# A four-layer graph network on one core: a first stage with a hand-written order, R held as two reduced-precision rows, both attention scores from one product

## The chip, the cores and the metric

The kernel runs on one core of one Trainium2 chip. The time is the device time of one execution in microseconds; of several runs the median is given. Every trace is that of one further, profiled execution, whose own time stands beside its span.

## What is computed

A stack of four layers over a graph of N = 3327 nodes with 512 features. The adjacency matrix is an N x N array of integers with about half a per cent of ones. Layers 0, 2 and 3 are graph attention with 8 heads of 64 features, layer 1 is a SAGE layer (mean of the neighbours); each is applied to relu(layernorm(x)) and added to x. Cut to what matters, a layer of attention is:

```python
h   = maximum(layernorm(x), 0)
Wh  = (h @ W).reshape(n, H, F)
f1  = einsum('nhf,hf->nh', Wh, a1)          # score of the destination
f2  = einsum('nhf,hf->nh', Wh, a2)          # score of the source
e   = leaky_relu(f1[:, None, :] + f2[None, :, :], 0.2)
e   = where(adj[:, :, None] > 0, e, -9e15)
out = einsum('ijh,jhf->ihf', softmax(e, axis=1), Wh)
x   = x + elu(out)                          # layer 0: batch norm and relu instead
```

and layer 1 is

```python
agg = mask @ h / maximum(deg, 1)
x   = x + relu(concat([h @ W_self + b_self, agg @ W_nb + b_nb]) @ W_comb + b_comb)
```

## The kernel before

Nodes are padded to 3328 and taken in 26 blocks of 128 rows; the destinations are taken in 52 groups of 64 (GB). Since few edges exist, each group has a list of source nodes, the union of the neighbours of its 64 nodes, and only those rows are gathered.

**A weight without the leaky relu.** Since exp(leaky_relu(f1 + f2)) is the larger of exp(f1 + f2) and exp(0.2 (f1 + f2)), a weight of the softmax is, up to a factor that the softmax removes, the larger of R(destination) = exp(0.8 f1 + a constant) and a value of the source, times exp(f2). exp(f2) is multiplied into the features beforehand. So a table row of a source (v_row, written to `table`) holds, for each head, exp(f2) x Wh, exp(f2) itself, and the value that is compared; `r_dram` holds R.

**The first stage** (0 to about 355 us) is the function `lists`, which also runs the projection of layer 0 (`Projection.block`, `Norms.block`) and the products of the weights with the attention vectors (`Products.layer`, L477 and L478). For each of the 26 blocks of rows of the adjacency matrix, DVE compares the integers with zero and counts them (L878, adj_b), PE packs them into words (26 small products, L882, words_ps), ACT copies the words (L883) and DVE takes two maxima (L885, which groups have which sources). After two of every three blocks one block of the projection follows: its normalisation (L764 to L770 on DVE, L779 on ACT), four transposes (L782, h_ps), relu (L785, hT), two score products (L593, with the destination scores as rows; L595 with the source scores as columns; sd_ps), the product with W (L597, wh_ps), the exponentials (L600, L601, L605), the clamp (L604) and the multiplication of a row (L610). After blocks 5 and 11 come the weight products of layers 2 and 3. Then the marks are transposed (L906 and L909, cnt), a scan (L912) and 11 steps, one for each bit (L918 to L921), turn them into lists of sources, each step followed by one of the remaining blocks of the projection; L926 and L927 end this. The lists go to DRAM and come back in another layout (L940 and L950, half on SP's queue, half on ACT's), and are put into an index array (L960 to L972). The first gather of layer 0 reads `idx` and `table`. What runs when on each engine is set by the scheduler here, which takes the order of the program as a guide.

**Attention** (`attend`, three times) has a fixed order on PE, DVE and ACT. The sources of a group come in units of three chunks of 128. POOL gathers rows for the next unit (L1019); for each group PE spreads R over the partitions (`spread`, L1052, r_bc: a product of a row of 512 with a column of ones), fetched two groups ahead on SP's queue (L1044, r_one); DVE takes the maximum (L1120, mx) and multiplies with the mask (L1127, wgt); PE accumulates the products of weights and rows (L1141, facc; about 110 a group). When a group is complete, `ending` divides and writes it out in steps, one step per unit (`later`), and the same call ticks whatever runs beside.

**Beside** layer 0 run products of weights for the later SAGE layer (fwx_ps, fb_ps) and sums for the batch norm (bmean_ps). Beside SAGE runs the projection of layer 2, beside layer 2's attention that of layer 3: class `Following`. Its `tick` advances the oldest block that is ready by one step, and all early ones (norm). A block has four steps in `rest`: transposes and relu (p_ps L710, hT L713); scores (p_sd, L717 and L719) with the exponentials L722 and L723 and a copy of the destination scores (L725); the clamp (L728) and the product with W (p_wh, L731); the exponential of R, its DMA and the multiplication of the rows (L733 to L739). All its tiles in PSUM share one tag with `pb` buffers, 2 beside SAGE and 1 beside layer 2's attention. What is left at the end of a stage is worked off by `drain`.

Of the kernel before, what the change touches and what calls it, by code (L numbers as in the profile page):

```python
# [24 lines left out]
BF16 = mybir.dt.bfloat16  # L25
I32 = mybir.dt.int32
# [10 lines left out]
P = 128  # L37
H = 8
F = 64
# [414 lines left out]
class Products:  # L454
# [4 lines left out]
    def __init__(self, tc, t, pool, wp, wps):  # L459
        self.nc, self.t, self.wp, self.wps = tc.nc, t, wp, wps  # L460
        self.WA = []
        for l in range(3):
            WA = pool.tile([P, KC, 2 * H], F32, name=f"WA{l}")
            self.WA.append(WA)
        self.ok = pool.tile([1, 1], I32, name="ok")

    def layer(self, l):
# [3 lines left out]
        nc.scalar.dma_start(Wt, t[wn].rearrange("(kc p) o -> p kc o", p=P))  # L471
        for k, an in enumerate((ai, aj)):
            ab = wp.tile([P, D], F32, name="wa_bc", tag="wa_bc", bufs=2)
            nc.scalar.dma_start(ab, t[an].partition_broadcast(P))
            for kc in range(KC):
                pr = wp.tile([P, D], F32, name="wa_pr", tag="wa_pr", bufs=2)
# [5 lines left out]
    def bound(self):  # L482
# [9 lines left out]
        ps = self.wps.tile([P, 3, 2 * H], F32, name="wa_n")  # L492
# [78 lines left out]
class Projection:  # L571
# [4 lines left out]
    last, pb = "wh_ps", 1  # L576

    def __init__(self, tc, cs, N, wl, xin, W, WA, table, r_dram, pool, psum, hb=2):
# [6 lines left out]
        self.norms = Norms(tc, cs, pool, psum, xin, hb)  # L585

    def block(self, c):
        nc, pp, pps, WA, wl = self.tc.nc, self.pool, self.psum, self.WA, self.wl
        hT = self.norms.block(c, self.hs)
        wh = pps.tile([P, D], F32, name="wh_ps", tag="wh_ps", bufs=1)  # L590
        sd = pps.tile([P, BANK], F32, name="sd_ps", tag="sd_ps", bufs=1)
        for kc in range(KC):
            nc.tensor.matmul(sd[:, :H], hT[:, kc, :], WA[wl][:, kc, H:], start=(kc == 0), stop=(kc == KC - 1))  # L593
        for kc in range(KC):
            nc.tensor.matmul(sd[:H, P : 2 * P], WA[wl][:, kc, :H], hT[:, kc, :], start=(kc == 0), stop=(kc == KC - 1))  # L595
        for kc in range(KC):
            nc.tensor.matmul(wh, hT[:, kc, :], self.Wt[:, kc, :], start=(kc == 0), stop=(kc == KC - 1))  # L597
        row = pp.tile([P, ROW], F32, name="v_row", tag="v_row", bufs=3)
        V = row[:, : H * (F + 1)].rearrange("p (h f) -> p h f", f=F + 1)
        nc.scalar.activation(V[:, :, F : F + 1], sd[:, :H].rearrange("p (h o) -> p h o", o=1), AF.Exp)  # L600
        nc.scalar.activation(row[:, H * (F + 1) :], sd[:, :H], AF.Exp, scale=-0.8, bias=self.cs["down"])  # L601

        rr = pp.tile([H, P], F32, name="r_row", tag="r_row", bufs=2)
        nc.vector.tensor_scalar(rr, sd[:H, P : 2 * P], -SMALL, SMALL, ALU.max, ALU.min)  # L604
        nc.scalar.activation(rr, rr, AF.Exp, scale=0.8, bias=self.cs["down"][:H])  # L605
        n = P // GB
        nc.sync.dma_start(
            self.r_dram[c * n : (c + 1) * n, :, :].rearrange("g h i -> h g i"), rr.rearrange("h (g i) -> h g i", i=GB)
        )
        nc.vector.tensor_tensor(  # L610
            V[:, :, 0:F], wh.rearrange("p (h f) -> p h f", f=F), V[:, :, F : F + 1].to_broadcast([P, H, F]), ALU.mult
        )
        nc.sync.dma_start(self.table[c * P : (c + 1) * P, :ROW], row.bitcast(I32))
# [39 lines left out]

class Following:
# [15 lines left out]
    def tick(self):  # L670
        if self.ready and next(self.ready[0], None) is None:
            self.ready.pop(0)
        for g in list(self.early):
            hx = next(g)
            if hx is not None:
                self.early.remove(g)
                self.ready.append(self.rest(*hx))
# [28 lines left out]
    def rest(self, c, hx):  # L706
# [9 lines left out]
        for kc in range(KC):  # L716
            nc.tensor.matmul(sd[:, :H], hT[:, kc, :], WA[wl][:, kc, H:], start=(kc == 0), stop=(kc == KC - 1))  # L717
        for kc in range(KC):
            nc.tensor.matmul(sd[:H, P : 2 * P], WA[wl][:, kc, :H], hT[:, kc, :], start=(kc == 0), stop=(kc == KC - 1))  # L719
        row = pp.tile([P, ROW], F32, name="v_row", tag="v_row", bufs=2)  # L720
        V = row[:, : H * (F + 1)].rearrange("p (h f) -> p h f", f=F + 1)
        nc.scalar.activation(V[:, :, F : F + 1], sd[:, :H].rearrange("p (h o) -> p h o", o=1), AF.Exp)  # L722
        nc.scalar.activation(row[:, H * (F + 1) :], sd[:, :H], AF.Exp, scale=-0.8, bias=self.cs["down"])  # L723
        rr = pp.tile([H, P], F32, name="r_row", tag="r_row", bufs=2)
        nc.scalar.copy(rr, sd[:H, P : 2 * P])  # L725
        yield True

        nc.vector.tensor_scalar(rr, rr, -SMALL, SMALL, ALU.max, ALU.min)  # L728
        wh = self.psum.tile([P, D], F32, name="p_wh", tag="p_ps", bufs=self.pb)
        for kc in range(KC):  # L730
            nc.tensor.matmul(wh, hT[:, kc, :], self.Wt[:, kc, :], start=(kc == 0), stop=(kc == KC - 1))  # L731
        yield True
        nc.scalar.activation(rr, rr, AF.Exp, scale=0.8, bias=self.cs["down"][:H])  # L733
        n = P // GB
        nc.sync.dma_start(
            self.r_dram[c * n : (c + 1) * n, :, :].rearrange("g h i -> h g i"), rr.rearrange("h (g i) -> h g i", i=GB)
        )
        for h in range(H):
            nc.scalar.mul(V[:, h, 0:F], wh[:, h * F : (h + 1) * F], V[:, h, F : F + 1])  # L739
        nc.sync.dma_start(self.table[c * P : (c + 1) * P, :ROW], row.bitcast(I32))  # L740
        yield None


class Norms:


    def __init__(self, tc, cs, pool, psum, xin, hb):
        self.__dict__.update(locals())
        self.NB = xin.shape[0] // P
        self.have = {}  # L750

# [726 lines left out]
```

## Time and profile before

| | us |
|---|---|
| three runs | 3010.09, 2994.06, 2988.13 |
| median | 2994.06 |
| the profiled execution, its own time | 3035.44 |
| its span, first to last instruction | 3033.2 |
| its mean granted TensorE clock | 0.788 |

| stage, from the trace | us |
|---|---|
| adjacency loop: first compare starts, last compare ends | 24.9, 252.3 |
| final shift of the lists ends (L927) | 338.3 |
| first gather of layer 0 | 355.4 |
| layer 0's attention | 355 to 945 |
| batch norm and own part of SAGE | 945 to 1120 |
| SAGE with the projection of layer 2 | 1120 to 1733 |
| layer 2's attention with the projection of layer 3 | 1733 to 2430 (from 2386 the drain) |
| layer 3's attention | 2440 to 3033 |

How to read the lines shown below. PE is TensorE (products), PEld its loading of weights, DVE VectorE, ACT ScalarE, POOL GpSimd, SP SyncE, which issues DMAs. A row of digits divides the span into 40 slices, and each digit is the busy share in tenths; PEclk is the clock that was granted to TensorE, in tenths of the full one. The chain of waits follows back from the last instruction what released each piece; "issue" is time in which an engine waited for nothing that the profile shows. A line of a group reads: line, engine, operation, output<-inputs, shapes, xcount, then busy time in us and the mean of one in ns, then the idle time of the engine before them and what ended it. A line of the waits reads: engine, its line, what it waited for, then us in total, number, longest. A line of the windows reads: window, its length, busy us (and number of instructions) of PE, PEld, DVE, ACT and POOL, then the clock, the DMA engines' share and GB/s.

### The profile page before, as it was taken

How to read it: one execution, taken by the hardware profiler on the slowest of the kernel's cores; microseconds unless marked ns; L12 is line 12 of the kernel's file. 1: busy time of each engine (PE TensorE's matmuls, PEld its weight loads, DVE VectorE, ACT ScalarE, POOL GpSimd, SP SyncE). 2: the span in 40 equal slices, each digit the busy share in tenths (PEclk: the TensorE clock that was granted, in tenths of full speed). 3: DMA queues.
4: the chain of work that ended last, by engine and by line, in shares of the span. 5: the costliest groups of instructions: out<-in, count | busy, mean ns of one | idle time of the engine just before them, and what ended most of it. 6: DMA issues, size and time to landing. Idle time of an engine off the chain costs nothing.

```text
span 3033.2 us, 55483 instructions
## 1 busy us (share of the span) xinstructions
PE 2335.1 (77%) x22046; PEld 1441.9 (48%) x22046; DVE 1797.3 (59%) x2124; ACT 1051.0 (35%) x3857; POOL 1376.2 (45%) x1464
## 2 busy tenths in 40 slices
PE   4767577878787786888988677888889757777775
PEld 2434244555554332333333355555665445656554
DVE  7657577778876910011111277777766367887886
ACT  1223112233334322344444313445666601223333
POOL 1000255556551046666554255555544056565553
PEclk9778788877778898799999767777777766676766
DMA  7563377776662746666655366666655166666664
GB/s 279 186 258 125 133 217 226 235 222 207 201 191 78 248 140 198 195 202 221 202 182 180 114 169 183 186 181 188 185 173 171 56 184 186 188 195 194 200 197 130
DMA packets 186637, 561.52 MB, mean 185 GB/s; under 512 B 35385, under 2 KB 40321, under 8 KB 183044
## 3 DMA queue, kind: packets, MB, share of 16 engines
q0 software_dynamic: 114880, 404.47, 45.4%
q1 hardware_dynamic: 68470, 148.32, 13.8%
q10 hardware_dynamic: 3022, 5.11, 0.5%
q8 instruction: 177, 2.90, 0.4%
q14 instruction: 88, 0.72, 0.1%
HBM read 498.42 MB, written 59.36 MB: 184 GB/s over the span
## 4 chain that ended last, share of the span: by engine, by line
PE 63%; issue 14%; ACT 5%; DVE 2%; another core or an unknown queue 2%; DMA 1%; POOL 1%; SPq 0%; DVEq 0%; ACTq 0%; POOLq 0%
PE facc L1141 29%; PE p_wh L731 7%; PE r_bc L1052 6%; PE sage_acc L1376 5%; PE n_ps L1325 3%; PE p_sd L719 2%; PE p_sd L717 2%; PE s_ps L1300 2%; PE fwx_ps L1218 1%; PE bmean_ps L1228 1%; PE p_ps L710 1%; ACT v_row L739 1%; POOL rows L1019 1%; PE a_ps L1319 1%
## 5 line engine op out<-in xcount | busy, mean ns | idle before, releaser
L1019 POOL DMA_INDIRECT rows<-table,idx x1077 | 1025.4, 952 | 1231.6 <-PE facc L1141 362.4
L1141 PE MATMUL facc<-rows,wgt 128*64 128x65 f32 x17232 | 953.3, 270 | 380.9 <-issue 342.1
L1141 PEld LDWEIGHTS facc<-rows,wgt 128*64 128x64 f32 x17232 | 826.1, 178 | 669.3 <-issue 556.4
L1127 DVE TENSOR_TENSOR wgt<-mx,mask 128x1536 f32<-128x1536 f32 (+1 forms) x405 | 638.3, 1576 | 174.4 <-PE facc L1141 82.4
L1120 DVE TENSOR_TENSOR mx<-r_bc,rows 128x1536 f32<-128x1536 f32 (+1 forms) x405 | 639.5, 1579 | 163.9 <-PE facc L1141 75.9
L1019 POOL DMA_INDIRECT z_rows<-h_dram,idx x359 | 341.2, 950 | 392.0 <-ACT hT L1297 139.2
L1079 ACT ACTIVATE fhp<-sums,rd 64x64 f32<-64x64 f32 x832 | 219.7, 334 | 146.9 <-DVE rd L1073 85.2
L1052 PE MATMUL r_bc<-r_one,fones 1*128 1x512 f32 x312 | 220.9, 793 | 15.8 <-DMA r_one<-r_dram 9.3
L731 PE MATMUL p_wh<-fWt,hT 128*128 128x512 f32 x416 | 215.3, 664 | 1.8 <-ACT r_row L725 1.8
L1376 PE MATMUL sage_acc<-z_rows,z_mask 128*64 128x512 f32 x718 | 208.4, 635 | 10.6 <-issue 6.2
L1069 ACT COPY sums<-facc 128x260 f32<-128x260 f32 x156 | 57.5, 368 | 405.8 <-PE facc L1141 344.9
L728 DVE TENSOR_SCALAR r_row<-r_row 8x128 f32<-8x128 f32 x52 | 11.8, 228 | 301.7 <-ACT r_row L725 183.7
L1112 ACT ACTIVATE mask<-on 128x192 uint8<-128x192 uint16 (+1 forms) x135 | 46.5, 344 | 394.9 <-DVE on L1106 202.6
L1330 DVE TENSOR_TENSOR s_o<-n_ps,bn_y 128x512 f32<-128x512 f32 x26 | 17.9, 687 | 209.9 <-PE n_ps L1325 185.4
L731 PEld LDWEIGHTS p_wh<-fWt,hT 128*128 128x128 f32 x416 | 85.3, 216 | 107.4 <-issue 101.6
L597 PE MATMUL wh_ps<-fWt,hT 128*128 128x512 f32 x208 | 124.7, 731 | 2.5 <-DVE v_row L610 2.5
L739 ACT ACTIVATE v_row<-p_wh,v_row 128x64 f32<-128x64 f32 x416 | 89.8, 322 | 80.4 <-PE p_wh L731 70.3
L1325 PE MATMUL n_ps<-fWx,aT 128*128 128x512 f32 x208 | 106.7, 651 | 5.1 <-ACT aT L1321 3.4
L1079 ACT ACTIVATE bn_y<-sums,rd 64x64 f32<-64x64 f32 x416 | 109.5, 333 | 2.4 <-DVE rd L1073 0.5
L1376 PEld LDWEIGHTS sage_acc<-z_rows,z_mask 128*64 128x64 f32 x718 | 51.0, 140 | 116.6 <-issue 103.0
L1300 PE MATMUL s_ps<-fWx,hT 128*128 128x512 f32 x208 | 95.8, 615 | 9.2 <-ACT hT L1297 9.2
L713 ACT ACTIVATE hT<-p_ps 128x128 f32<-128x128 f32 x208 | 54.6, 277 | 123.2 <-PE facc L1141 82.8
(191 smaller groups left out, 2153.8 us busy)
## 6 DMA issues: line engine op xcount, KB each, us to landing
adj_i<-in_adj SPq DMA_DIRECT2D x26, 1664.0 KB
table<-v_row SPq DMA_DIRECT2D x78, 264.0 KB
rows<-table,idx POOLq DMA_INDIRECT x1077
fin_x<-fx SPq DMA_DIRECT2D x52, 256.0 KB
ln_x<-in_x SPq DMA_DIRECT2D x26, 256.0 KB
bn_x<-in_x SPq DMA_DIRECT2D x13, 512.0 KB
fx<-bn_x SPq DMA_DIRECT2D x13, 512.0 KB
fsage_x<-fx SPq DMA_DIRECT2D x26, 256.0 KB
```

Source lines behind the costliest of these rows:

```text
L597: nc.tensor.matmul(wh, hT[:, kc, :], self.Wt[:, kc, :], start=(kc == 0), stop=(kc == KC - 1))
L731: nc.tensor.matmul(wh, hT[:, kc, :], self.Wt[:, kc, :], start=(kc == 0), stop=(kc == KC - 1))
L739: nc.scalar.mul(V[:, h, 0:F], wh[:, h * F : (h + 1) * F], V[:, h, F : F + 1])
L1019: nc.gpsimd.indirect_dma_start(out=dst, out_offset=None, in_=src[:, :], in_offset=bass.IndirectOffsetOnAxis(ap=idx[:, k : k + 1], axis=0))
L1052: nc.tensor.matmul(rb, ones[0:1, :], rrs.pop(g), start=True, stop=True)
L1079: nc.scalar.mul(hp[o0 : o0 + GB, h * F : (h + 1) * F], sm[mine, q, 0:F], rd[mine, q, :])
L1120: nc.vector.tensor_tensor(mx[:, :n], rbs[g].unsqueeze(1).to_broadcast(full), gt[:, :n, H * (F + 1) : ROW].unsqueeze(3).to_broadcast(full), ...
L1127: nc.vector.tensor_tensor(wt[:, :n], mx[:, :n], mk.unsqueeze(2).to_broadcast(full), ALU.mult)
L1141: nc.tensor.matmul(accs[g][v * GB : (v + 1) * GB, q * (F + 1) : (q + 1) * (F + 1)], wt[:, k, h, :], gt[:, k, h * (F + 1) : (h + 1) * (F + 1)],
L1300: nc.tensor.matmul(ps, hT[:, kc, :], Wx[:, 0, kc, :], start=(kc == 0), stop=(kc == KC - 1))
L1325: nc.tensor.matmul(ps, aT[:, kc, :], Wx[:, 1, kc, :], start=(kc == 0), stop=(kc == KC - 1))
L1376: nc.tensor.matmul(acc[u * GB : (u + 1) * GB, :], m, z, start=f, stop=l)
```

## The change

- **The first stage** has a fixed order on PE, DVE and ACT. `Projection` is cut in four turns that work on different blocks: in one call the multiplication of a row and R's second half for the block three back, the norm, and the transposes and relu for the block one back (`first`); then the normalisation on ACT, the transpose of R for the block three back, scores and product with W for the block two back, and statistics for the block five ahead (`second`). The comparison of block c + 1 is put after the words of block c. The weight products are spread over the blocks, and their loads move from ACT's to SP's queue. The 11 bit steps alternate with the remaining half turns.
- **Scores.** One product with all 16 columns gives both scores as columns; the one with the scores as rows is dropped, here and in `Following`. R is then computed as a column (`halves`) and transposed on PE.
- **R in two rows.** R is rounded to the reduced FP32 type (F32R) as a first row, and the remainder is the second. `r_dram` holds both. `spread` is one product of two rows with ones, in that type.
- **`Following`** has six steps instead of four (transpose and copy of R are new), and `tick` takes up to two steps when two or more blocks are ready.
- The second half of the lists (list_b) goes by POOL's DMA queue instead of ACT's.

```diff
@@ Products.layer
-        nc.scalar.dma_start(Wt, t[wn].rearrange("(kc p) o -> p kc o", p=P))
+        nc.sync.dma_start(Wt, t[wn].rearrange("(kc p) o -> p kc o", p=P))
...
             for kc in range(KC):
+                yield
@@ Projection (block and Norms are replaced)
+    def first(self):
+        nc, pp, p = self.tc.nc, self.pool, self.turns
+        if 0 <= p - 3 < self.NB:
+            c = p - 3
...
+            nc.vector.tensor_tensor(
+                V[:, :, 0:F], wh.rearrange("p (h f) -> p h f", f=F), V[:, :, F : F + 1].to_broadcast([P, H, F]), ALU.mult
+            )
+            nc.sync.dma_start(self.table[c * P : (c + 1) * P, :ROW], self.row.pop(c).bitcast(I32))
+            self.r[c] = self.r[c]()
+        self.norms()
+        if 0 <= p - 1 < self.NB:
+            c = p - 1
+            tp = self.psum.tile([P, KC, P], F32, name="h_ps", tag="h_ps", bufs=self.hb)
+            for kc in range(KC):
+                nc.tensor.transpose(tp[:, kc, :], self.have[c][0][:, kc * P : (kc + 1) * P], self.cs["ident"])
...
+    def second(self):
...
+        if p < self.NB:
+            xt, rs, ng = self.have[p]
+            nc.scalar.activation(xt, xt, AF.Identity, scale=rs, bias=ng)
+        if 0 <= p - 3 < self.NB:
+            c = p - 3
+            tr = pps.tile([2 * H, P], F32, name="tr_ps", tag="sd_ps", bufs=2)
+            nc.tensor.transpose(tr, self.r.pop(c), self.cs["ident"])
+            rr = pp.tile([2 * H, P], F32, name="r_row", tag="r_row", bufs=2)
+            nc.scalar.copy(rr, tr)
...
+        if 0 <= p - 2 < self.NB:
+            c = p - 2
...
+            for kc in range(KC):
+                nc.tensor.matmul(sd, hT[:, kc, :], WA[wl][:, kc, :], start=(kc == 0), stop=(kc == KC - 1))
+            wh = pps.tile([P, D], F32, name="wh_ps", tag="wh_ps", bufs=2)
...
+            sf = pp.tile([P, H], F32, name="s_col", tag="s_col", bufs=2)
+            nc.vector.tensor_scalar(sf, sd[:, :H], -SMALL, SMALL, ALU.max, ALU.min)
+            self.wh[c], self.row[c], self.r[c] = wh, row, halves(nc, pp, self.cs, sf)
+        self.stats(p + LNB)
+def halves(nc, pool, cs, sf):
+    rf = pool.tile([P, H], F32, name="r_full", tag="r_full", bufs=2)
+    rs = pool.tile([P, 2, H], F32, name="r_half", tag="r_half", bufs=2)
+    nc.scalar.activation(rf, sf, AF.Exp, scale=0.8, bias=cs["down"])
+    nc.scalar.copy(rs.bitcast(F32R)[:, 0, :], rf)
+    def other():
+        nc.vector.tensor_tensor(rs.bitcast(F32R)[:, 1, :], rf, rs[:, 0, :], ALU.subtract)
+        return rs.rearrange("p t h -> p (t h)")
+    return other
@@ Following.tick
-        if self.ready and next(self.ready[0], None) is None:
-            self.ready.pop(0)
+        for _ in range(min(2, len(self.ready))):
+            while self.ready and next(self.ready[0]) is None:
+                self.ready.pop(0)
@@ Following.rest
-            nc.tensor.matmul(sd[:, :H], hT[:, kc, :], WA[wl][:, kc, H:], start=(kc == 0), stop=(kc == KC - 1))
-        for kc in range(KC):
-            nc.tensor.matmul(sd[:H, P : 2 * P], WA[wl][:, kc, :H], hT[:, kc, :], start=(kc == 0), stop=(kc == KC - 1))
+            nc.tensor.matmul(sd[:, : 2 * H], hT[:, kc, :], WA[wl][:, kc, :], start=(kc == 0), stop=(kc == KC - 1))
...
+        yield True
+        tr = self.psum.tile([2 * H, P], F32, name="p_tr", tag="p_ps", bufs=self.pb)
+        nc.tensor.transpose(tr, rs(), self.cs["ident"])
+        yield True
+        rr = pp.tile([2 * H, P], F32, name="r_row", tag="r_row", bufs=2)
+        nc.scalar.copy(rr, tr)
...
@@ lists
+            for c in range(NB):
+                on = c % 3 < 2
+                if on:
+                    proj.first()
+                gathered(c)
+                if on:
+                    proj.second()
+                compare(c + 1)
+                next(more, None)
...
+            close = closing()
+            next(close)
+            while proj.left():
+                proj.first()
+                next(close, None)
+                proj.second()
+                next(close, None)
...
-            eng = (nc.sync, nc.scalar)[i]
+            eng = (nc.sync, nc.gpsimd)[i]
...
-        with tc.tile_pool(name="lset2_ps", bufs=2, space=PSUM) as lps:
+        with tc.tile_pool(name="lset2_ps", bufs=1, space=PSUM) as lps:
@@ attend
-                    rr = ap.tile([1, H * GB], F32, name="r_one", tag="r_one", bufs=3)
-                    nc.sync.dma_start(rr, r_dram[g : g + 1, :, :].rearrange("g h i -> g (h i)"))
+                    rr = ap.tile([2, H * GB], F32, name="r_two", tag="r_two", bufs=3)
+                    nc.sync.dma_start(rr, r_dram[g, :, :, :].rearrange("t h i -> t (h i)"))
...
-                    nc.tensor.matmul(rb, ones[0:1, :], rrs.pop(g), start=True, stop=True)
+                    nc.tensor.matmul(rb, ones[0:2, :].bitcast(F32R), rrs.pop(g).bitcast(F32R), start=True, stop=True)
```

In `lists`, gathered(c) holds the words, their copy and the maxima of block c, compare(c) its load and comparison, and closing() the cnt products, the scan, the bit steps and the final shift; their instructions are those of before. Tiles in PSUM: the words, cnt and the check of the weights share two banks, the scores and R's transposes two, wh_ps two (before one), h_ps one.

## The prediction

> **What bounds the kernel.** First the page's totals and chain: what ended last.
>
> ```profile
> PE   4767577878787786888988677888889757777775
> PEclk9778788877778898799999767777777766676766
> ...
> PE 63%; issue 14%; ACT 5%; DVE 2%; another core or an unknown queue 2%; DMA 1%; POOL 1%; SPq 0%; DVEq 0%; ACTq 0%; POOLq 0%
> ...
> L1141 PE MATMUL facc<-rows,wgt 128*64 128x65 f32 x17232 | 953.3, 270 | 380.9 <-issue 342.1
> ...
> L1052 PE MATMUL r_bc<-r_one,fones 1*128 1x512 f32 x312 | 220.9, 793 | 15.8 <-DMA r_one<-r_dram 9.3
> ```
>
> PE and its unexplained gaps ("issue", nearly all before facc) hold 77% of the chain, and r_bc is 221 us of PE work. But is a microsecond of PE work a microsecond of time? Second, the busy time by stage (first stage to the last compare, its closing part, layer 0, SAGE, layers 2 and 3):
>
> ```profile
> core 0: us, PE busy (x) PEld busy (x) DVE busy (x) ACT busy (x) POOL busy (x), PEclk, DMA share, GB/s
> 0.00:252.00 252.00, 156.30 (x1145) 95.68 (x1146) 164.07 (x337) 56.36 (x240) 9.57 (x28) 0.82 0.64 238
> 252.00:355.00 103.00, 80.40 (x362) 45.62 (x361) 72.36 (x114) 23.47 (x113) 0.00 (x0) 0.88 0.21 64
> 355.00:945.00 590.00, 452.41 (x5970) 304.29 (x5970) 455.68 (x458) 173.08 (x600) 340.01 (x359) 0.77 0.69 214
> ...
> 1120.00:1733.00 613.00, 506.63 (x1807) 212.32 (x1805) 64.91 (x164) 240.67 (x992) 331.11 (x349) 0.90 0.60 185
> 1733.00:2430.00 697.00, 566.39 (x6537) 390.04 (x6538) 474.33 (x477) 335.49 (x1275) 333.29 (x349) 0.76 0.57 165
> 2440.00:3033.00 593.00, 429.43 (x5844) 329.70 (x5844) 458.93 (x373) 161.27 (x520) 333.82 (x350) 0.67 0.64 183
> ```
>
> Layer 0 carries about 97 us of PE work (fwx_ps 44.5, bmean_ps 40.7, fb_ps 11.2) that layer 3 lacks, and takes the same 590 us: slope zero, with a clock of 0.67 where PE does less. Layer 2 has 137 us more than layer 3 and takes 104 more; without its 39 us of drain (which holds some 30 us of PE work), 65 for about 107: slope 0.6. SAGE is PE at 83%. Third, the waits of the first 360 us:
>
> ```profile
> POOL rows L1019 <- SPq L1474: 345.2, 1, 345.2
> ACT words L883 <- PE words_ps L882: 95.6, 20, 28.3
> PEld L882 <- DVE adj_b L878: 69.1, 15, 28.6
> ACT v_row L600 <- PE sd_ps L595: 64.3, 24, 5.8
> ACT hT L785 <- PE h_ps L782: 44.0, 19, 9.8
> DVE r_row L604 <- ACT v_row L601: 43.2, 19, 6.1
> ```
>
> The stage gates layer 0 (the first gather starts at 355.4), yet PE is 62% and DVE 65% busy in its loop: a ring of waits, each engine waiting for the next, no full engine.
>
> **What the Trainium skill says.** "FP8 and Floating Point Precision", TensorE Precision Notes: true FP32 takes four passes, "FP32 reduced precision" reads FP32 and truncates. The trace has r_bc as two records per group (312 for 156 groups); no record here shows a reduced one. "TensorE: Matmul & The Clock Gate", Part 1: PE runs at half clock after an idle window of about 3.4 us; the PEclk row agrees in kind (0.67 in layer 3, 0.90 in SAGE). "DMA: Bandwidth & Descriptors", SWDGE vs HWDGE vs iDMA: a DMA issued from GpSimd is written by software, and slower to set up than from SP or ACT; the gather's issue here takes 0.95 + 0.30 us on POOL.
>
> **Part 1, the first stage by hand.** Rows used:
>
> ```profile
> L878 DVE TENSOR_SCALAR_CACHE_REDUCE adj_b<-adj_i 128x3328 bf16<-128x3328 int32 x26 | 93.7, 3603 | 2.7 <-DMA adj_i<-in_adj 2.7
> ...
> L597 PE MATMUL wh_ps<-fWt,hT 128*128 128x512 f32 x208 | 124.7, 731 | 2.5 <-DVE v_row L610 2.5
> ...
> L595 PE MATMUL sd_ps<-hT,WA 128*8 128x128 f32 x208 | 36.3, 329 | 0.0
> ```
>
> (The other durations are from the same view of groups.) DVE sum of the new loop: 26 compares at 3.60 + 0.08 + 0.14 = 99; 52 maxima at 0.26 = 14; 24 products at 0.68 + 0.67 = 32, 8 of them before the loop; 26 statistics at 0.83 = 22; 18 row multiplies at 0.68 = 12; norms and small ones about 15; first compare at 24.9. Floor of the loop's end: 25 + 194 - 11 = 208. A PE turn with a block (h_ps, 26 words products 0.87, one transpose, one score product, wh) is about 6 us at full clock and 11 at half; 18 of those and 8 bare turns at 5 give 238 cold. I take 228, 24 earlier than the last compare now (252.3). L595 goes: 26 x 8 x 0.174 = 36 us of PE, hidden in the ring. The adjacency (26 x 1.70 MB), x and the weights, some 52 MB, must come in 203 us, 256 GB/s; the page's first slice moves 279, so just covered; if not, compares wait and the lower bound is gone.
>
> The fixed order also adds waits. On PE the words products stand behind h_ps, which waits for ACT's normalised block; behind them stand transpose, scores and wh, and for wh waits v_row, the head of DVE's next turn, with the next compare behind it. Each of these takes data from one to three turns back, so I put them at nothing, covered by the 3.8 us compare; with that cover gone, h_ps costs up to what ACT waits for it now, 44 us, which is in the cold end of the range.
>
> Closing: now 258.2 to the final shift at 338.3, 80 us, a block in each of eight bit steps. New: cnt about 7, the scan turn 6.6, five turns with two bit steps (2 x 3.62 + 1.0 = 8.2 each, 41), the last 8.5, waits 5: 68, so 12 less. Behind it four turns of projection remain (5 each, 20, mean 5, table write 5: 30), beside list_b, whose 15 DMAs move to POOL's queue: 15 x 1.25 = 19 against 5.8 for twelve on ACT's queue, then about 11 as now. Both ways 30, against 17.1 from shift to first gather now: 13 lost. On SP's queue the weight loads and list_a's shift DMAs now stand among table writes; the row DMAs split in 32 pieces instead of 8: at nothing, under the turns. Sum **-24**; range -50 (turns on the floor) to +10 (cold turns, POOL tail 20 longer).
>
> **Part 2, r_bc by one reduced-precision product of two rows.** Now 220.9 / 156 = 1.42 us a group. One record of the same 512 columns in one pass instead of two: 0.40 (793 / 2); saved 1.02 x 156 = 159. If it costs a full record, 97; below nothing it can't go while the record is no longer than two were. Realised at a slope between 0 and 0.6 (the stages above; I let it reach 0.9): 0.4, **-64**; range 0 to -143. The load of two rows has the same issue on SP, two groups ahead: nothing.
>
> **Part 3, one score product in Following.**
>
> ```profile
> L719 PE MATMUL p_sd<-hT,WA 128*8 128x128 f32 x416 | 75.9, 342 | 0.9 <-issue 0.8
> ```
>
> It goes: 1.46 us a block. Added: p_tr, by the nearest row (p_ps transposes, 326 ns) 0.33. Net 1.13 x 26 = 29 in each stage. SAGE (slope 0.8, its PE share): **-23**, range -35 to 0. Layer 2: -18 by slope 0.6; but two steps a tick put p_ps and p_sd back to back for about 15 blocks, through one PSUM buffer (pb=1), so PE waits for ACT's four hT copies (4 x 0.277 = 1.1): +17. facc and the group's ending queue behind that wait. Net **-1**, range -25 to +20. ACT's added exponential and copies (about 0.8 a block) hide in its 52% idle of layer 2; SAGE likewise.
>
> Sum -24 - 64 - 23 - 1 = **-112** on the profiled execution's 3035 us, which is 41 (1.4%) above the median of the runs; scaled, 2994 - 110 = **2884**.
>
> **Rivals.**
> *Full PE-bound* (0.13): every PE microsecond counts. For it: 77% of the chain. Against: layer 0 beside layer 3. -40 - 143 - 29 - 18 = -230: 2767.
> *The spread saves nothing* (0.18): the gaps called "issue", or DVE (77% busy in layers 0 and 3), set a group's period. For it: 110 us of issue in layer 0 and 135 in layer 3 before facc. Only parts 1 and 3: -48: 2946.
> *It doesn't do what it says* (0.08): the two-row product runs in as many passes, so PE saves nothing there: 2946 to 2960.
> *Slower by the clock* (0.11): in the three attention layers, PE with less work falls to half clock for longer. facc took 290 us busy in layer 2 at 0.76 but 360 in layer 3 at 0.67, for the same products. PE busy without r_bc there: 452 + 566 + 429 - 214 = 1233 (214 = r_bc in these windows) at a mean clock of 0.735. At 0.65 that becomes 1394, +161, against -112: about 3042. It is over 1% slower from 1233 x (0.735/k - 1) > 142, k below 0.66. Against: the gaps are shorter than the groups that they stand in, and a shorter group fills them.
>
> **The numbers.** Forecast 0.50, own range 2830 to 2940. One per cent, 30 us, is about what a measurement can tell. Faster: 0.49 + 0.13 + 0.11 + 0.04 = 0.77; within 1%: 0.01 + 0.07 + 0.04 + 0.02 = 0.14; slower 0.09. The range leaves out the clock rival above and the lower half of the PE-bound one below: 2785 to 2975.
>
> **What would show it.** Part 1: last compare near 228, final shift near 300, first gather near 330; a first gather after 355 refutes it. Part 2: 156 records of r_bc near 0.4 us; layers 0 and 3 some 20 us shorter each; unchanged layers with less r_bc mean the second rival; 312 records, or 0.8 us, the third. Part 3: no L719-like product, SAGE near 590, waits of p_sd for hT near 1 us each in layer 2. A PEclk in layer 3 below 0.6 with longer facc records is the clock rival.

## The result, and the profile after

The change made the kernel faster by about one per cent: 2967.88 us (four runs, 2963.61 to 2969.83) against 3000.98 us for the kernel before (four runs); ratio 0.9891, 95% interval 0.9846 to 0.9936. The forecast was 110 us; 33 us came. The profiled execution of the changed kernel took 2969.83 us, span 2967.7.

The later runs were made under one of two conditions, and this must be known to read them. Under one, that of the result above, the kernel before takes 3000 to 3033 us; call it **A**. Under the other, **B**, the same kernel takes 2580 us. What makes the condition is not known. The runs bear chip numbers, and number 11 stands both on runs under B (`e1`, `e2`, `e3`, `e10`) and on runs under A (`e4`, `e7`, `e11`, `e12`), so A and B are not shown to be two kinds of chip, as some of the expectations below call them. Every comparison with the kernel before stays within one condition. On A the changed kernel was faster three times (ratios 0.9891, 0.9926, 0.9908). On B it is slower: 2595.87 against 2579.85 us, ratio 1.0072 (1.0045 to 1.0100).

The page of the changed kernel, the rows that answer to those shown before (clock, chain, facc, spread):

```profile
PE   2677577877675985888999567878777657677775
PEclk9778798867778997889999777877777766775655
...
PE 57%; issue 15%; ACT 8%; another core or an unknown queue 4%; DVE 3%; DMA 2%; POOL 0%; SPq 0%; DVEq 0%; ACTq 0%; POOLq 0%
...
L1228 PE MATMUL facc<-rows,wgt 128*64 128x65 f32 x17232 | 982.1, 268 | 411.2 <-issue 399.1
```

The spread, in the view of groups of the same kernel, and the stages in the view of windows (loop and closing part of the first stage, layer 0, SAGE, layers 2 and 3):

```profile
L1139 PE MATMUL r_bc<-r_two,fones 2*128 2x512 f32 x156 | 95.6, 617 | 12.9 <-issue 5.4 <-DMA r_two<-r_dram 4.5 <-PE facc L1228 2.1
```

```profile
0.00:221.00 221.00, 123.75 (x1001) 76.83 (x1001) 175.12 (x347) 55.78 (x258) 11.48 (x31) 0.79 0.74 275
221.00:330.00 109.00, 84.05 (x325) 46.55 (x324) 71.32 (x133) 29.96 (x147) 7.60 (x15) 0.85 0.18 53
330.00:909.00 579.00, 417.70 (x5926) 292.32 (x5924) 455.94 (x460) 174.35 (x604) 340.51 (x359) 0.80 0.72 218
...
1087.00:1683.00 596.00, 486.80 (x1573) 188.02 (x1572) 64.05 (x187) 247.88 (x1044) 328.28 (x347) 0.90 0.62 190
1683.00:2376.00 693.00, 514.64 (x6350) 369.43 (x6350) 480.05 (x505) 340.55 (x1327) 334.48 (x352) 0.77 0.59 168
2386.00:2967.00 581.00, 409.27 (x5794) 335.39 (x5794) 458.77 (x373) 161.46 (x520) 333.88 (x350) 0.64 0.67 187
```

The reader is to see that r_bc fell from 220.9 to 95.6 us of busy time (half the records, 617 ns instead of 793), while the idle time before facc that is put down to nothing ("issue") rose from 342.1 to 399.1 and facc's own busy time from 953.3 to 982.1. PE has less to do and waits more. A single facc product did not take longer (268 ns instead of 270): the busy time counts overlapping products once, so it can grow when they overlap less.

The stages, from the first and last facc and sage_acc products of each trace (layer 2 with its drain, to layer 3's first product). The trace of the kernel before on A is of an execution 34 us longer than the median of its runs; in the set of runs that `e15` belongs to, the kernel before takes 3032.96 us, so the third column is the fairer one to compare it with:

| us | A: before | A: after | A: after, `e15` | B: before (`e3`) | B: after (`e19`) |
|---|---|---|---|---|---|
| span | 3033.2 | 2967.7 | 3003.5 | 2577.4 | 2590.3 |
| first facc | 371.0 | 346.0 | 345.2 | 370.0 | 346.7 |
| layer 0 | 574.2 | 561.4 | 566.8 | 470.0 | 468.7 |
| first sage_acc to layer 2 | 650.0 | 638.9 | 662.2 | 544.5 | 542.8 |
| layer 2 with its drain | 710.3 | 702.9 | 704.0 | 562.7 | 601.4 |
| layer 3 | 571.1 | 560.4 | 567.7 | 472.7 | 473.8 |

The first stage gave its 23 to 26 us under both conditions. Layers 0 and 3 gave 3 to 13 us each on A and nothing on B. Layer 2 gave 6 to 7 us on A and **lost 39 us on B**.

### The profile page after: what moved, and what is told of

Read it like the earlier page. It is cut to its first block, busy times and chain, and to the rows that moved or that the text cites. A ratio compares the mean times of both kernels' runs of the same rounds, so it can differ in the third digit from the quotient of the medians.

```text
span 2967.7 us, 54270 instructions
## 1 busy us (share of the span) xinstructions
PE 2177.8 (73%) x21344; PEld 1372.4 (46%) x21344; DVE 1813.4 (61%) x2208; ACT 1069.6 (36%) x4013; POOL 1384.6 (47%) x1482
## 4 chain that ended last, share of the span: by engine, by line
PE 57%; issue 15%; ACT 8%; another core or an unknown queue 4%; DVE 3%; DMA 2%; POOL 0%; SPq 0%; DVEq 0%; ACTq 0%; POOLq 0%
PE facc L1228 29%; PE p_wh L823 7%; PE sage_acc L1463 5%; PE n_ps L1412 3%; PE r_bc L1139 3%; PE p_sd L810 2%; PE s_ps L1387 2%; ACT v_row L827 2%; PE bmean_ps L1315 1%; ACT fhp L1166 1%; PE fwx_ps L1305 1%; DVE mx L1207 1%; PE p_ps L803 1%; ACT hT L806 1%
## 5 line engine op out<-in xcount | busy, mean ns | idle before, releaser
L1228 PE MATMUL facc<-rows,wgt 128*64 128x65 f32 x17232 | 982.1, 268 | 411.2 <-issue 399.1
L1463 PE MATMUL sage_acc<-z_rows,z_mask 128*64 128x512 f32 x718 | 229.0, 655 | 9.6 <-DMA z_rows<-h_dram,idx 8.9
L823 PE MATMUL p_wh<-fWt,hT 128*128 128x512 f32 x416 | 227.1, 693 | 1.4 <-ACT s_col L817 1.4
L820 DVE TENSOR_SCALAR s_col<-s_col 128x8 f32<-128x8 f32 x52 | 9.9, 190 | 303.3 <-ACT s_col L817 125.6
L1027 POOL DMA_DIRECT2D list_b<-shift x12 | 6.0, 504 | 277.7 <-DVE shift L983 277.7
L810 PE MATMUL p_sd<-WA,hT 128*128 128x16 f32 x416 | 74.7, 304 | 65.4 <-ACT hT L806 57.0
L810 PEld LDWEIGHTS p_sd<-WA,hT 128*128 128x128 f32 x416 | 71.2, 245 | 99.1 <-ACT hT L806 68.0
```

The source lines that it names most:

```text
L810: nc.tensor.matmul(sd[:, : 2 * H], hT[:, kc, :], WA[wl][:, kc, :], start=(kc == 0), stop=(kc == KC - 1))
L1228: nc.tensor.matmul(accs[g][v * GB : (v + 1) * GB, q * (F + 1) : (q + 1) * (F + 1)], wt[:, k, h, :], gt[:, k, h * (F + 1) : (h + 1) * (F + 1)],
L1463: nc.tensor.matmul(acc[u * GB : (u + 1) * GB, :], m, z, start=f, stop=l)
```

## The experiments

### What the spread's saving is worth

Undone in the changed kernel (`e1`), doubled (`e2`), and done alone on the kernel before (`e10`); with them the kernel before for a second trace (`e3`). All four on B.

```diff
 e1
-  nc.tensor.matmul(rb, ones[0:2, :].bitcast(F32R), rrs.pop(g).bitcast(F32R), start=True, stop=True)
+  nc.tensor.matmul(rb, ones[0:2, :], rrs.pop(g), start=True, stop=True)
 e2
+  for _ in range(2):
       nc.tensor.matmul(rb, ones[0:2, :].bitcast(F32R), two.bitcast(F32R), start=True, stop=True)
 e10, on the kernel before
-  nc.tensor.matmul(rb, ones[0:1, :], rrs.pop(g), start=True, stop=True)
+  nc.tensor.matmul(rb, ones[0:1, :].bitcast(F32R), rrs.pop(g).bitcast(F32R), start=True, stop=True)
```

> The changed kernel with the spread of R back in full FP32 (two rows, the same data), nothing else. Theory of supply (what sets a group's period is the rate at which PE gets through its many short facc instructions, and a long instruction beside them is nearly free): r_bc takes about 1.4 us a group again, +125 us of PE work in all, but the time rises by only 20 to 40 us, near the kernel before minus its first stage (about 2995). Theory of a full PE: +90 to +125 us, 3060 or more.

> The changed kernel with the reduced-precision spread issued twice into the same tile, so one more instruction of 512 columns a group. Theory of supply: +95 us of PE work cost 10 to 30 us (2978 to 2998). Theory of a full PE: +80 to +95 (3050 to 3065).

> The kernel before once more, for a second trace of it. The trace in hand ran 3035 us against a median near 3000. If its extra 35 us are spread over the attention layers (clock or supply), then those layers are some 10 us shorter here and the difference to the changed kernel in them nearly vanishes; the first stage should be the same to 2 us (first gather near 355).

> The kernel before with its one-row spread taken as one reduced-precision product: part 2 alone, with R truncated to that type and the remainder left out. Theory of supply: 15 to 35 us shorter than before (about 2965 to 2985). Theory of a full PE: 100 to 125 us shorter (below 2900).

Measured: before 2579.34 us; `e1` 2616.20, ratio 1.0129 (1.0099 to 1.0159); `e2` 2598.69, ratio 1.0072 (1.0049 to 1.0094); `e10` 2569.42, ratio 0.9955 (0.9935 to 0.9975). The expected absolute times meant A and do not apply, and `e3`, a single run, cannot say where the first trace's extra 35 us lay. Against the changed kernel on B (2595.87, measured at another time), `e1`'s 115 us more of r_bc cost 20 us, nearly all in layer 2 (625.6 instead of 601.4), and `e2`'s second product 3 us, which the intervals cannot tell from nothing. The trace of the kernel before on B says why. Its chain, and facc in the view of groups:

```profile
PE 35%; DVE 24%; issue 10%; DMA 7%; ACT 6%; POOL 3%; DVEq 0%; SPq 0%; POOLq 0%; ACTq 0%
```

```profile
L1141 PE MATMUL facc<-rows,wgt 128*64 128x65 f32 x17232 | 730.0, 255 | 309.1 <-DVE wgt L1127 212.1 <-issue 69.5 <-ACT sums L1069 14.8
```

PE has 35% of the chain instead of 63%, and facc waits for DVE's weights (212.1 us), not for nothing (69.5 instead of 342.1). On B layers 0 and 3 are DVE's: 470 and 473 us, of which DVE is busy 449 and 455. PE work saved there is saved beside DVE.

The same on A: part 2 alone on the kernel before (`e18`; `e13` is the same kernel again on B), and undone where layer 2 has no other waits (`e17`, on top of `e7` below).

> Part 2 alone once more (the kernel before with the one-row spread in reduced precision), for a chip of the other kind. Where before takes about 3000 us: if gaps of fixed number set PE's pace, 5 to 20 us shorter than before, with some 130 us less r_bc; if PE's work does, 60 us or more. Where it takes about 2580: 10 us shorter, as before.

> Part 2 alone on the kernel before (one row in reduced precision). Where before takes about 3000 us: 5 to 20 us shorter if gaps set PE's pace, 60 us or more if PE's work does. Where it takes about 2580: 10 us shorter, as twice before.

> The changed kernel with the following projection's steps set apart (as in the run that did this alone) and the spread back in full FP32: part 2 undone where layer 2 has no waits on its one PSUM buffer. Theory that r_bc is nearly free: within 12 us of the same kernel with the reduced spread (2958 on the slower kind of chip, about 2550 on the faster). Rival, a PE-bound layer 2: 20 us or more longer, all of it in layer 2.

Measured: `e13` (B) 0.9959 (0.9941 to 0.9977). `e18` (A) 3005.39 against 3032.96 us, ratio 0.9897 (0.9869 to 0.9924): 28 us for 130 us of PE work, a slope of 0.21; its stages are shorter by 7 (layer 0), 22 (layer 2) and 0 us (layer 3), for 42 to 44 us of r_bc saved in each. That is between the two expectations. `e17` (A) 2976.91; `e7` took 2958.17 on A at another time: 19 us for 133, a slope of 0.14, of which layer 2 has 13. That is outside the 12 us and just short of the 20. So the price depends on the stage: about 0.3 to 0.5 of the saved work in layer 2, 0 to 0.2 in layers 0 and 3. Where the rest goes is seen on facc of `e18`, in the view of groups:

```profile
L1141 PE MATMUL facc<-rows,wgt 128*64 128x65 f32 x17232 | 981.5, 268 | 460.9 <-issue 421.7 <-DVE wgt L1127 29.4 <-DMA rows<-table,idx 1.9
```

The issue gaps rose by 80 us (342.1 to 421.7) and facc's busy time by 28 (953.3 to 981.5): 108 of the 130 us came back around the same products, each of which takes no longer (268 ns against 270).

### What sets the pace of an attention layer

DVE's work halved (`e4`, on A), facc narrowed (`e5`, on B) and facc thinned out (`e6` on B, `e16` on A).

```diff
 e4: the maximum is written into wgt, the mask is left out
-  nc.vector.tensor_tensor(mx[:, :n], ..., ALU.max)
-  nc.vector.tensor_tensor(wt[:, :n], mx[:, :n], mk.unsqueeze(2).to_broadcast(full), ALU.mult)
+  nc.vector.tensor_tensor(wt[:, :n], ..., ALU.max)
 e5
+  lo = 0 if f else 48
-  gt[:, k, h * (F + 1) : (h + 1) * (F + 1)],
+  gt[:, k, h * (F + 1) + lo : (h + 1) * (F + 1)],
 e6, e16
-  for q in range(hq):
+  for q in range(hq if f or l else 1):
```

> The changed kernel without the multiplication with the mask: DVE writes the maximum straight into the weights (left out: the zeros at non-neighbours), so DVE's work in an attention layer is about halved, PE's is the same. Where DVE sets a group's period: layers 0 and 3 shorter by 60 us or more each. Where PE's gaps set it: less than 15 us each.

> The changed kernel with facc's products narrowed to 17 of the 65 columns in all chunks but the first of a group (left out: the sums of 48 features of those chunks); the number of PE instructions is unchanged. If the chip is one where before takes about 3000 us: if the number of instructions sets the pace, layers 0 and 3 stay within 15 us of 567; if PE's time in the array sets it, they fall by 50 us or more, towards DVE's 470. Where before takes about 2580 us, no effect over 5 us (DVE sets the pace there).

> The changed kernel with facc's products for only 2 of the 8 heads in the chunks between a group's first and last (left out: the others' sums there; the copy of the sums adds a small constant, so that no sum is zero). PE's instructions in an attention layer fall to about 47 per cent, DVE's work is the same. Where before takes about 3000 us: layers 0 and 3 fall from 567 to between 470 and 500 whichever of the two sets the pace, and the unexplained gaps before facc fall at least in proportion. Where before takes about 2580: under 10 us.

> Once more the kernel with facc's products for only 2 of 8 heads between a group's first and last chunk (the others' sums left out there, a small constant added). Where before takes about 3000 us: layers 0 and 3 fall from 567 to between 470 and 500, and the gaps before facc put down to issue fall from about 150 us a layer to under 75. If they stay near 567, neither the number of PE's instructions nor PE's work sets the pace, but something beside both (DMA or the gathers). Where before takes about 2580: no effect over 5 us in layers 0 and 3.

`e4`: 2999.84 us where the changed kernel took 3012.86; layers 0 and 3 at 565.7 and 567.4 instead of 570.5 and 566.9. Half of DVE's work gone, and at most 5 us gained in a layer: on A DVE is not the pace.

`e16`: 2874.86 us, ratio 0.9476 (0.9446 to 0.9507); layers 0 and 3 at 530.0 and 533.4 instead of 566.8 and 567.7. Half of facc gone brought 35 us a layer, not the 70 to 100 expected. The gaps put down to issue even grew in sum. Waits in layer 3 of the changed kernel, then of `e16` (total, number, longest):

```profile
PE facc L1228 <- issue: 156.4, 320, 10.7
```

```profile
PE facc L1228 <- issue: 215.0, 230, 3.7
```

But this sum mixes two things. Some of these gaps end within 0.3 us after the end of a weight multiplication on DVE, so they are probably waits for DVE that the profile does not name: in layer 3 of `e16` 116 of the 215 us, in that of `e15` (the changed kernel) 13 of 160, and on B all of them (39 gaps, 74.4 us, in `e19`). Without them the gaps of the three attention layers fall from 715 (352 us) in `e15` to 351 (229 us) in `e16`, their number about in step with facc's instructions (47%), while `e4` with half of DVE's work keeps them (718, 372 us). On B, in `e3`, `e6` and `e19`, there is not one. So these gaps belong to A and go with the number of PE's instructions, which fits the theory of supply (the rate at which PE gets through its many short instructions sets the pace) without proving it. Its forecast for the layer's time failed all the same: in `e16` waits for DVE came forward and the clock in layer 3 fell to 0.50 (`e15`: 0.68), and what each of the two cost is not told apart.

How they look, in layer 3 of `e15`, PE in order of time:

```profile
2608.89 0.27 PE L1228 MATMUL facc<-rows,wgt 128*64 128x65 f32 x1 [0.95 <-issue]
2609.62 0.27 PE L1228 MATMUL facc<-rows,wgt 128*64 128x65 f32 x1 [0.47 <-issue]
2610.35 0.37 PE L1228 MATMUL facc<-rows,wgt 128*64 128x65 f32 x1 [0.46 <-issue]
2611.06 0.27 PE L1228 MATMUL facc<-rows,wgt 128*64 128x65 f32 x1 [0.34 <-issue]
2611.82 4.37 PE L1228 MATMUL facc<-rows,wgt 128*64 128x65 f32 x74 [0.49 <-issue]
```

For a while a product starts only every 0.7 us or so, and then 74 follow without a gap. What holds PE there stays open. It is not that single transfers take longer: in layer 3 a packet of the gathers takes 191 ns on average on A (`e15`) and 187 on B (`e19`), and one of the queue that the trace names "instruction" 1.03 and 1.11 us.

`e6` on B: ratio 1.0028 (1.0015 to 1.0041), layers 0 and 3 at 467.4 and 471.9: DVE's pace, as expected. `e5` on B was a miss: **slower**, 2679.51 us, ratio 1.0395 (1.0369 to 1.0421), layer 0 at 510.0 and layer 2 with its drain at 649.1, though layer 3 stayed at 472.7. PE in its layer 0, in order of time, and the windows of the same kernel:

```profile
601.92 3.60 PE L1229 MATMUL facc<-rows,wgt 128*64 128x17 f32 x64
605.46 0.79 PE L1139 MATMUL r_bc<-r_two,fones 2*128 2x512 f32 x1
```

```profile
400.00:800.00 400.00, 381.44 (x4625) 282.58 (x4623) 347.16 (x352) 134.60 (x471) 262.73 (x278) 0.50 0.78 242
```

64 narrow products take 3.60 us, 56 ns each. Wide ones, 48 at a time in layer 3 of the changed kernel on B (`e19`), take 60 ns each at a clock of 0.50 and 34 at 1.00:

```profile
2204.59:2207.46 2.87, 2.86 (x48) 2.67 (x48) 2.77 (x2) 0.00 (x0) 2.26 (x3) 0.50 0.79 246
2212.02:2213.64 1.62, 1.61 (x48) 1.48 (x48) 1.62 (x1) 0.00 (x0) 1.31 (x2) 1.00 0.74 222
```

So at the same clock the missing 48 columns saved about 4 ns of 60, and what was lost is the clock: it is 0.50 over these 400 us of `e5`, where `e19` has 0.86 in layer 0, and the other products of that layer are slower too (fwx_ps 1142 ns instead of 690). PE is busy for 381 of 400 us and became the bound. That the weight loads, unchanged at 64 columns, set the time of a narrow product fits (64 of them took 3.50 us in the same stretch), but was not tried by itself. Why the clock fell is not shown. It fell in `e6` too, whose products are wide but half as many: 0.60 in layer 0 and 0.50 in layer 3, against 0.86 and 0.71 in `e19`.

### The waits that layer 2 gained

The changed kernel on B, PE in layer 2 in order of time (start, length, then in brackets the idle time before and what ended it); before it the same stretch of the kernel before:

```profile
1912.77 1.12 PE L1052 MATMUL r_bc<-r_one,fones 1*128 1x512 f32 x2
1913.82 2.55 PE L1141 MATMUL facc<-rows,wgt 128*64 128x65 f32 x80
1916.30 0.66 PE L710 MATMUL p_ps<-fident,ln_h 128*128 128x128 f32 x4
1916.89 1.12 PE L1052 MATMUL r_bc<-r_one,fones 1*128 1x512 f32 x2
1917.94 1.62 PE L1141 MATMUL facc<-rows,wgt 128*64 128x65 f32 x48
1919.49 1.06 PE L717 MATMUL p_sd<-WA,hT 128*128 128x8 f32 x8
```

```profile
1916.82 0.28 PE L831 MATMUL p_tr<-fident,r_half 128*16 128x128 f32 x1
1917.02 1.15 PE L1228 MATMUL facc<-rows,wgt 128*64 128x65 f32 x32
1920.68 0.66 PE L803 MATMUL p_ps<-fident,ln_h 128*128 128x128 f32 x4 [2.50 <-ACT r_row L834]
1922.56 1.89 PE L810 MATMUL p_sd<-WA,hT 128*128 128x16 f32 x8 [1.23 <-ACT hT L806]
1924.38 0.79 PE L1139 MATMUL r_bc<-r_two,fones 2*128 2x512 f32 x1
```

There are two waits in most blocks, not one. The copy of R out of PSUM ends a block's steps, and `tick` goes on at once to the next block's transposes, which need the one buffer that this copy empties: 2.50 us. Then the scores stand right behind those transposes: 1.23 us. In layer 2 of this trace they sum to 37.8 us (16 times) and 20.9 us (17 times), where the kernel before on B waits 12.6 and 4.2 us before the same products. On A the shares are turned round, 14.5 and 46.0 us, for ACT is late with hT there, up to 4.1 us; the view of groups in layer 2 of the changed kernel on A:

```profile
L810 PE MATMUL p_sd<-WA,hT 128*128 128x16 f32 x208 | 43.5, 341 | 52.1 <-ACT hT L806 46.0 <-issue 6.0
L803 PE MATMUL p_ps<-fident,ln_h 128*128 128x128 f32 x104 | 21.0, 335 | 24.8 <-ACT r_row L834 14.5 <-issue 9.7 <-ACT fin_x L1257 0.6
```

`e7` (on A) sets both apart in one change, so it does not tell what each of the two is worth:

```diff
 Following
+  def more(self):
+      if len(self.ready) > 1:
+          self.tick(1, False)
-  while self.ready and next(self.ready[0]) is None:
+  if self.ready and next(self.ready[0]) is None:
 attend, in the loop over a unit's chunks; layer 2 ticks one step at a time
+  if k == 1:
+      more()
```

`e11` (and `e14` on B) adds a mended tail of the first stage: both lists on POOL's queue, and the check of the weights ahead of the last turns.

```diff
-  eng = (nc.sync, nc.gpsimd)[i]
+  eng = nc.gpsimd
...
+  if proj.left() == 9:
+      prods.bound(lps, "words_ps")
```

> The changed kernel again, beside the kernel before on the same chip. In the chip's run where before took 2579 us, the attention layers had hardly any unexplained gaps on PE and lasted as long as DVE's work (470 us in layers 0 and 3). If this chip is of that kind: first gather 25 us earlier, layers 0 and 3 equal to within 3 us, SAGE equal, layer 2 with its drain 40 to 50 us longer than before's 563, so the whole 10 to 20 us (0.4 to 0.8 per cent) slower than before. If it is of the first kind (before near 3000): 30 us faster, as before.

> The changed kernel with the steps of the following projection set apart in layer 2: one step at a time, the second of a unit between two chunks of facc, and the copy of R as a step of its own, so that neither the scores stand right behind their transposes nor the next transposes right behind the copy of R. Theory that the waits on the one PSUM buffer (2.3 us of p_ps for the copy of R, 1.2 us of p_sd for hT, about 16 blocks) make layer 2 longer: these waits go, layer 2 with its drain is 35 to 50 us shorter than in the changed kernel. Rival, that DVE's or ACT's added work makes it longer: less than 10 us shorter.

> As the run before it, and in the closing part of the first stage all list DMAs on POOL's queue and the check of the weights ahead of the last turns, so that list_a no longer stands behind table<-mean on SP's queue. Theory: idx is ready 6 to 10 us earlier (first gather near 322 instead of 331), nothing else changes. Rival, that the mean's product or the table's writes end the stage anyway: under 3 us.

> The changed kernel with the steps of the following projection set apart and the lists on POOL's queue, once more, for a chip of the other kind. Where before takes about 2580 us: layer 2 with its drain at 555 to 575 instead of 610, so the whole 15 to 35 us shorter than before (0.6 to 1.4 per cent). Where it takes about 3000: 2.5 to 3 per cent shorter, as in the run before.

Measured on A, before at 3032.06 us: the changed kernel (`e12`) 3012.86, ratio 0.9926 (0.9898 to 0.9954); `e7` 2958.17, ratio 0.9741 (0.9707 to 0.9775); `e11` 2946.49, ratio 0.9725 (0.9699 to 0.9751). Layer 2 with its drain: 704.6, 656.5 and 659.6 us. In `e7`'s layer 2 the wait for the copy of R is down to 4.0 us and that for hT to 9.9 (R's transpose now waits 12.5 us for ACT), and the stage is 48 us shorter. On B `e14` took 2544.05, ratio 0.9869 (0.9850 to 0.9888), with layer 2 at 565.4 instead of 601.4. **With most of both waits gone, the kernel beats the one before under both conditions.** The tail of the lists gave less than expected: the first gather was to come near 322 us and came at 326.8 in `e11`, against 329.4 to 333.3 in three traces on A with the first stage unmended (`e7`, the result, `e12`). `idx` was written from 324.2 us, instead of 328.1 in `e7` and 330.3 in the result. The times of `e7` and `e11` overlap, so only the traces show it.

Three more runs: the changed kernel again (`e15` on A, `e19` on B), and the dropped score product put back, unread, on top of `e7` (`e20`, B).

```diff
 e20
+  for kc in range(KC):
+      nc.tensor.matmul(sd[:H, P : 2 * P], WA[wl][:, kc, :H], hT[:, kc, :], start=(kc == 0), stop=(kc == KC - 1))
```

> The changed kernel once more. Where before takes about 2580 us: first gather 25 us earlier, layers 0, 3 and SAGE as before within 3 us, layer 2 with its drain 35 to 48 us longer than 563, so the whole 8 to 22 us slower than before. Where before takes about 3000: 20 to 35 us faster, layer 2 near 704.

> The changed kernel. Where before takes about 2580 us: 8 to 20 us slower than before, all of it layer 2 (35 to 48 us longer with its drain) less the first stage (25 us). Where before takes about 3000: 20 to 35 us faster, as three times before.

> The changed kernel with the following projection's steps set apart, and the dropped score product put back beside the new one (nobody reads it): 26 x 8 more records in SAGE and in layer 2, some 30 us of PE work each. If PE's work is the pace: SAGE 25 and layer 2 15 to 30 us longer than without it. If the work hides in gaps or beside DVE: under 10 us each. On a chip where before takes about 2580 us, where SAGE's PE has hardly a gap, SAGE should show it in full (20 to 30 us).

`e15`: 3006.17, ratio 0.9908 (0.9877 to 0.9939). `e19` is the B measurement given with the result. `e20`: 2557.46, ratio 0.9916 (0.9891 to 0.9941); SAGE takes 550.2 us, 11 more than in `e14` and 7 more than in `e19`, and layer 2 with its drain is not longer (562.9 against 565.4). The product put back is 58.3 us of busy PE time over both stages. Of its half in SAGE about a third shows, where 20 to 30 us were expected; of that in layer 2 nothing does.

## Why the prediction was off

Three terms failed. The spread was priced at one slope of 0.4 for all its stages: -64 was said, -19 to -28 came. SAGE was to give 23 us and gave none that is seen. In layer 2 the waits of the double steps were counted for one product of a block where two wait, so that part 3 there cost about 15 us on A instead of gaining 1. These miss 36 to 45, 23 and about 16 us, and the forecast missed 77.

**Part 1, the first stage: right in sum, partly by luck.** -24 was said, 23 to 26 came. The last compare was to be near 228, and it ended at 219.9; the final shift near 300, and it ended at 290; the first gather near 330, and it came at 331.6. So the loop ended 8 to 10 us better and the tail was 12 us longer than said, and the two errors cancelled. The tail's wait was named wrongly. POOL's twelve list DMAs, costed at 1.25 us each, took 0.5 and were out by 296. A part of the tail was held by SP's queue, whose moves had been put "at nothing, under the turns". SP's issues in order of time:

```profile
308.91 0.88 SPq L1027 DMA_DIRECT2D list_a<-shift  x3
321.79 0.74 SPq L702 DMA_DIRECT2D table<-mean  x1
322.90 1.28 SPq L1027 DMA_DIRECT2D list_a<-shift  x4
```

The last four DMAs of list_a stood behind the mean's write, which waited 11.8 us for ACT. `e11`, which takes this wait away, had `idx` 4 to 6 us earlier, half of the 12 at most; what holds the rest of the tail was not traced.

**Part 2, the spread: the work fell as said, the slope was wrong.** Predicted were 0.40 us for a record, measured 0.61, so 125 us of PE work saved instead of 159. "FP8 and Floating Point Precision" of the Trainium skill (TensorE Precision Notes) has true FP32 take four passes and the reduced type truncate its operand. No trace shows passes, but less work for the reduced type agrees in kind: with the same two rows `e17` has 312 records of 804 ns in FP32, `e7` 156 of 589 ns in the reduced type. "Realised at a slope between 0 and 0.6 ... 0.4, -64" is the term that failed: `e18` and `e17` put it at 0.14 to 0.21 on A, 19 to 28 us, and `e10` at 0.09 on B. The two slopes that the 0.4 stands between were each right for their own stage only: layer 2 returned 0.3 to 0.5 of the work saved in it, near the 0.6 read there, and layers 0 and 3 returned 0 to 0.2, near the 0 read from comparing them (a comparison in which the clock differed too, 0.77 and 0.67). Two thirds of the saving lay in layers 0 and 3. The rival that the spread saves nothing, at 2946 us, was nearest to the 2968 measured; that gaps outlast the saving is what A shows (80 of the 130 us came back as gaps in `e18`), and that DVE sets the period is what B shows.

**Part 3 in SAGE: not seen.** -23 was said, at a slope equal to PE's share of the time; over three traces on A the stage took 639 to 663 us against 650, and on B 2 us less. `e20` prices the dropped product at 7 to 11 us on B, for 29 us of PE work.

**Part 3 in layer 2: the mechanism right, half of it missed.** "Net -1" was said; with the spread's gain set apart (`e18` on A, `e10` on B) layer 2 became 14 to 16 us longer on A and 41 on B. "PE waits for ACT's four hT copies (4 x 0.277 = 1.1): +17" came as 20.9 us on B (1.23 a block), but as 46.0 on A, where ACT comes to the copies late. The other wait, the next block's transposes for the copy of R (14.5 us on A, 37.8 on B), was missed: the reading stopped at the two steps of one block and did not follow `tick` over the end of a block into the next. Setting both apart brought 48 us on A and, with the tail of the lists, 36 in layer 2 on B.

With the measured terms on A, -25 for the first stage, -19 to -28 for the spread, about 0 for SAGE and +15 for part 3 in layer 2, the sum is -29 to -38. The result has -33; `e12` and `e15` have -19 and -27.

**The clock rival** did not come: layer 3's clock was 0.64 in the result's trace and 0.68 in `e12` and `e15`, against 0.67 before, and a facc product took no longer. "TensorE: Matmul & The Clock Gate" of the Trainium skill, Part 1, says that PE falls to half the clock after an idle window. No run here shows that: `e5`, with 0.50 while PE was busy for 381 of 400 us, is the case where a half clock did decide, and there PE did not stand idle.

## What to carry to other kernels

Before a microsecond saved on the busiest engine is counted, find its price stage by stage, from two stretches that differ in that work alone, and do not average the prices: here one stage returned up to half of the saving and two returned almost nothing. When gaps are put down to nothing, sort them by what ended just before, because some are waits that the profile does not name. When steps of a side task share one buffer, write out the order over the seam between two items as well, because that is where the end of one meets the start of the next. And a change that trades work for waits can turn its sign with the condition it runs under: where PE had gaps anyway it was a gain of a per cent, where it had none a loss.

## What was not expected of the hardware

The same kernel takes 2580 us under one condition and 3030 under the other, at granted clocks of 0.857 and 0.788. The first stage does not differ (first facc at 370 and 371 us), nor does the stretch between layer 0 and SAGE (136 and 135 us). All the difference is in the stages with gathers: 470 against 574 us in layer 0, 544 against 650 in SAGE, and the like in layers 2 and 3. In the attention layers it goes with gaps on PE that B does not have, that stay when DVE's work is halved (`e4`), and whose number halves with facc's instructions (`e16`). What makes PE wait there was not found, nor whether it lies in the chip or in something around it; no run here tried the gathers or the supply of instructions by themselves. How few columns a product has to have before PE no longer gains from fewer, and what lowers its clock then, is likewise open; 17 in place of 65 was too few.
